# Score shift as a DMA into the queries' row, the second product ahead of it, and one power for two norms

## The chip, the cores and the metric

One core of a Trainium2 chip runs the whole kernel in one launch. The metric is the device time of an execution in microseconds (us). In the profile PE is the matrix engine, PEld its weight loads, DVE the vector engine, ACT the scalar engine, POOL the GpSimd engine, and SP the engine that here only issues DMAs. An engine's name with a q (SPq, ACTq) stands for its instruction queue.

## The reference

Four sequences of 512 tokens with 512 features go through a gated block: attention of the tokens to themselves and to a second sequence (the context), both with queries from the tokens, and then a feed-forward part. The inputs are normed twice in a row, by the block's layer norm and by that of the attention:

```python
x = x + jnp.tanh(g_xattn[0]) * _L0_xattn_ref(_layernorm(x), ctx_2048, ...)
x = x + jnp.tanh(g_ffn[0]) * _L0_ffn_ref(_layernorm(x), w_gate_up, w_down)

def _layernorm(x, axis=-1, eps=1e-05):            # the first norm
    m = jnp.mean(x, axis=axis, keepdims=True)
    v = jnp.var(x, axis=axis, keepdims=True)
    return (x - m) / jnp.sqrt(v + eps)

# in _L0_xattn_ref: d = 128, g = 8 groups of 2 query heads, s = 512
ln_out = _ln(hidden_states, ln_w, ln_b)           # the second norm, eps 1e-5 too
q = _ln(_fp8_linear_pertensor(ln_out, wq, ...).reshape(b, s, g, hpg, d), qln_w, qln_b)
k = _ln(_fp8_linear_pertensor(ln_out, wk, ...).reshape(b, s, g, d), kln_w, kln_b)
v = _fp8_linear_pertensor(ln_out, wv, ...).reshape(b, s, g, d)
core = _gqa(q, k, v).reshape(b, s, nh * d)        # the same with qx and the context's kx, vx: xout
catq = _div_clamp_fp8(jnp.concatenate([core, xout], axis=-1), proj_smooth)
return jnp.einsum('bsi,oi->bso', catq, wproj) * (proj_in_scale * proj_w_scale)

def _gqa(q, k, v):
    scores = jnp.einsum('bsghd,btgd->bghst', q, k) / np.sqrt(q.shape[-1])
    return jnp.einsum('bghst,btgd->bsghd', jax.nn.softmax(scores, axis=-1), v)
```

The feed-forward part (a projection to 2 x 2048, a silu gate, a projection back, with weights of three values) is not touched by the change.

## The kernel before

The attention is cut into 64 blocks: a kind (0 self, 1 cross), a group of two heads and a sequence. Each block has two units, one for each head; a unit is one of the 128 **steps** of the main loop, and a step has two **halves**, of 256 queries each. There are 256 halves. The projections for later blocks run in the same halves: a `Pair` is two of a block's four token tiles, and one pair is projected in each step, five steps ahead.

The scores are kept exact enough by splitting queries and keys into a high and a low fp16 part. `qk` holds, for each token tile, seven turned chunks of 128 features: two query heads and the key in high parts (0 to 2), the same in low parts (3 to 5), and the key's high part again (6). Feature 0 is kept free: row 0 of chunk 6 is all ones, so whatever stands in row 0 of a low query chunk is added to all scores of that query. This row takes minus the largest score, so the exponential can be taken without overflow and without a pass of its own.

One half `n` of a step, in the order in which `step` writes it (u0 is the unit of this half, u1 that of the half before, u2 that of two halves before; w1, w2 are projected tiles on their way):

- `scores`: eight products of PE into `ps_s` (four key tiles by 256 queries, two terms). `ps_s` has two buffers.
- `shift_put` of u1: ACT copies the shift row from `mt` in PSUM to row 0 of the query chunk.
- `top`: DVE reduces the scores over the four key tiles to `mx` (128 x 256).
- `out` of w2 (ACT and DVE norm a projected tile into `z`), `sq` of w1 (ACT sums squares into `ss`).
- `shift_mm` and `exps` of u1: four products add the low queries and the shift; ACT takes the exponential of `ps_s` into `pt`.
- `pv` of u2: the second product, into `po`.
- `top_turn`: PE turns `mx` into `mt`.
- `vals` and `var` of w1 (ACT copies the values to `vv`; DVE, then POOL's power at L559, make `ss` the reciprocal deviation), and the next tile's projections (`mm`, into `ps_p`).
- `split`, once a step: ACT casts `z` to the high part in `hl`, POOL subtracts for the low part (L586), SP issues the transpose into `qk` (L587).
- `quant` and `turn_out`, once a step: DVE quantizes `ob`, SP transposes it into `ot` (L709), and ACT stores an earlier one to `cat_d`.
- `shift`: DVE reduces `mt` to `nm`, the negated maxima, with queries on partitions. `shift_row`: two products of PE with `nm`, broadcast, turn it into a row in `mt`.
- `evac` of u2: DVE scales `po` into `ob`.

The matrix, vector and scalar engines keep this written order from step 19 (`cfg["p0"]`) to the fourth step from the end; before and after that the build orders instructions by its own estimate of times. SP and POOL are ordered by the build throughout. Other work is hung into the halves by fixed lists (`PLAN`): each entry advances a generator by one step at a given point. The lists `a1`, `a2` and `a3` advance `prep_self`, which loads a sequence (`xt`), norms it, turns it and quantizes it into `xa` and `yx` (`yb` holds the scaled values). `prep_cross` does the same for the context: SP loads `cf` (L438), POOL subtracts (L447). After the attention come the output projection (`psj`, part of it early) and the feed-forward part (`ga`, `ub`, `psd`). Line 86 of the profile is a helper that issues all instructions of PE, DVE and ACT, so tiles are named rather than lines.

Of the kernel before, what the change touches and what calls it, by code (L numbers as in the profile page):

```python
# [22 lines left out]
NT = S // 128  # L23
# [71 lines left out]
def flamingo_kernel(  # L95
# [190 lines left out]
    with attn as ph:  # L286
# [11 lines left out]
        z_tiles = [nk.tile([128, 2, 3, 128], F32, name=f"z{i}") for i in range(2)]  # L298
        for t in z_tiles:
            gp.memset(t[:, :, 0:2, 0:1], 1.0)  # L300
        hl_tiles = [nk.tile([128, 2, 7, 128], F16, name=f"hl{i}") for i in range(2)]
        for t in hl_tiles:
            gp.memset(t[:, :, 6, 0:1], 1.0)
# [17 lines left out]
        def prep_self(b):  # L321
# [15 lines left out]
            t2 = sm.tile([128, 5, NT], F32, name="t21")  # L337
            v.tensor_scalar(t2[:, 0], mv[:, :, 1], EPS, None, ALU.add)
            gp.tensor_tensor(t2[:, 1], t2[:, 0], mhalf4, ALU.pow)
            yield  # L340
            v.tensor_tensor(t2[:, 2], t2[:, 1], t2[:, 1], ALU.mult)
            yield
            v.tensor_tensor(t2[:, 2], t2[:, 2], mv[:, :, 1], ALU.mult)
            yield
            v.tensor_scalar(t2[:, 2], t2[:, 2], EPS, None, ALU.add)
            gp.tensor_tensor(t2[:, 3], t2[:, 2], mhalf4, ALU.pow)
            yield
            v.tensor_tensor(t2[:, 3], t2[:, 3], t2[:, 1], ALU.mult)
            yield
            v.scalar_tensor_tensor(t2[:, 4], mv[:, :, 0], -1.0, t2[:, 3], ALU.mult, ALU.mult)  # L350
            yield
            for tt in range(NT):
                r, m = t2[:, 3, tt : tt + 1], t2[:, 4, tt : tt + 1]
# [147 lines left out]
        class Block:  # L501
            def __init__(self, ty, g, b):
                self.ty, self.g, self.b = ty, g, b
                self.qk = qkp.tile([128, NT, 7, 128], F16, name="qk")
                self.v = v_tiles[n_blocks[0] % 4]
                n_blocks[0] += 1

        class Pair:
# [55 lines left out]
            def out(self, i):  # L564

                ty, ps, z, r = self.ty, self.ps[i], self.z[:, i], self.ss[:, i, 2]
# [12 lines left out]
            def split(self, low=None):  # L579
                z, hl = self.z, hl_tiles[self.k % 2]  # L580
                gp.tensor_tensor(  # L581
                    z[:, :, 2, 0:1], self.acc, cb[:, self.ty : self.ty + 1].broadcast_to((128, 2, 1)), ALU.add
                )
                sc.copy(hl[:, :, 0:3], z)
                gp.tensor_copy(hl[:, :, 6, 1:128], z[:, :, 2, 1:128])
                (low or gp).tensor_tensor(hl[:, :, 3:6], z, hl[:, :, 0:3], ALU.subtract)  # L586
                sy.dma_start_transpose(  # L587
                    self.qk[:, self.pr * 2 : self.pr * 2 + 2].rearrange("p t c q -> p (t c) q"),
                    hl.rearrange("p i c d -> p (i c d)"),
                )  # L590

        class Unit:
# [9 lines left out]
            def scores(self, h):  # L602
                qk, j = self.blk.qk, self.j
                ps = self.ps[h] = pp_s.tile([128, NT, 256], F32, name="ps_s")
                for t in range(NT):
                    for n, (kc, qc) in enumerate(((2, j), (5, j))):
# [3 lines left out]
                            qk[:, t, kc],  # L610
                            qk[:, 2 * h : 2 * h + 2, qc],
# [5 lines left out]
            def top(self, h):  # L617
# [4 lines left out]
                v.tensor_reduce(self.mx, self.ps[h].rearrange("p t q -> p q t"), AX.X, ALU.max)  # L622

            def top_turn(self):
                mt = pp_o.tile([128, 512], F32, name="mt", tag="rb", bufs=1)
                self.mt = mt[:, 0:128].bitcast(F16).rearrange("p (i q) -> p i q", i=2)
                self.mr = mt[:, 128:384]
# [7 lines left out]
            def shift_row(self):  # L635

                mr = self.mr
                for i in range(2):
                    pe.matmul(
                        mr[:, i * 128 : i * 128 + 128],  # L640
                        self.nm[:, i : i + 1].broadcast_to((128, 128)),
                        ident16,
                        start=True,
                        stop=True,
                    )

            def shift_put(self, h):

                sc.copy(
                    self.blk.qk[0:1, 2 * h : 2 * h + 2, self.j + 3], self.mr[0:1].rearrange("p (i q) -> p i q", i=2)  # L650
                )

            def shift_mm(self, h):
                qk, ps = self.blk.qk, self.ps[h]
                for t in range(NT):
                    pe.matmul(
                        ps[:, t],
                        qk[:, t, 6],
                        qk[:, 2 * h : 2 * h + 2, self.j + 3],
# [145 lines left out]
        def step(s, k):  # L805
# [4 lines left out]
            for h in range(2):  # L810
# [7 lines left out]
                if u1:  # L818
                    u1.shift_put(h1)
# [421 lines left out]
```

## Time and profile before

| | |
|---|---|
| time, median of 3 runs | 1761.86 us (1759.51 to 1761.88) |
| profiled execution, its own time | 1761.26 us |
| span of that execution | 1759.5 us, 40972 instructions |
| PE busy | 1672.0 us (95%) |
| DVE busy | 1324.2 us (75%) |
| ACT busy | 1052.5 us (60%) |
| POOL busy | 569.0 us (32%) |
| DMA moved | 192.25 MB |

The profile is of one execution; 1.8 us of its time lie outside the span. An engine's busy share says how long it worked, not whether the end waited for it. The chain of waits follows the work that ended last back to the start and gives each engine and tile its share of that chain. In a line of the timeline the first number is the start in us from the start of the span, the second the duration in us, then the engine, the line, the instruction, what it writes and reads, and in brackets how long the engine had been idle and who released it. In a line of the chain the second number is the time by which that work moved the end. A line of waits gives who waited for whom, the total in us, the number of times and the longest. A line of DMA issues gives the destination and source, the queue, the count, KB each, and the median time in us from issue to landing.

### The profile page before, as it was taken

How to read it: one execution, taken by the hardware profiler on the slowest of the kernel's cores; microseconds unless marked ns; L12 is line 12 of the kernel's file. 1: busy time of each engine (PE TensorE's matmuls, PEld its weight loads, DVE VectorE, ACT ScalarE, POOL GpSimd, SP SyncE). 2: the span in 40 equal slices, each digit the busy share in tenths (PEclk: the TensorE clock that was granted, in tenths of full speed). 3: DMA queues.
4: the chain of work that ended last, by engine and by line, in shares of the span. 5: the costliest groups of instructions: out<-in, count | busy, mean ns of one | idle time of the engine just before them, and what ended most of it. 6: DMA issues, size and time to landing. Idle time of an engine off the chain costs nothing.

```text
span 1759.5 us, 40972 instructions
## 1 busy us (share of the span) xinstructions
PE 1672.0 (95%) x15174; PEld 1422.4 (81%) x15174; DVE 1324.2 (75%) x3967; ACT 1052.5 (60%) x3413; POOL 569.0 (32%) x725
## 2 busy tenths in 40 slices
PE   3589888999999999999999999999999999999999
PEld 2478787999999999999999999999999987443444
DVE  7888877777777778777777777777766665679876
ACT  6655555666666667666666666666665553457443
POOL 3453333334444335543333333333333330110000
PEclk8699999999999999999999999999999999999999
DMA  4433434344544455644445544544476664984333
GB/s 149 118 67 67 85 68 86 67 89 83 97 86 83 87 91 136 142 85 103 103 103 103 109 103 109 103 109 103 91 127 115 138 130 134 290 251 114 84 72 90
DMA packets 450312, 192.25 MB, mean 109 GB/s; under 512 B 417312, under 2 KB 421440, under 8 KB 447680
## 3 DMA queue, kind: packets, MB, share of 16 engines
q1 hardware_dynamic: 366688, 141.38, 38.7%
q10 hardware_dynamic: 82992, 44.07, 9.2%
q0 software_dynamic: 432, 4.19, 1.3%
q8 instruction: 119, 1.95, 0.4%
q14 instruction: 81, 0.66, 0.1%
HBM read 84.71 MB, written 23.09 MB: 61 GB/s over the span
## 4 chain that ended last, share of the span: by engine, by line
PE 82%; DVE 9%; ACT 3%; POOL 2%; DMA 2%; issue 1%; ACTq 0%; SPq 0%; DVEq 0%; POOLq 0%
PE ps_p L86 26%; PE po L86 23%; PE ps_s L86 17%; PE psj L86 5%; PE psd L86 3%; PE mt L86 3%; PE ub L86 3%; PE ga L86 3%; DVE mx L86 1%; DVE yb L86 1%; POOL ss L559 1%; DVE ob L86 1%; ACT z L86 1%; DMA ot<-ob 1%; DVE z L86 1%
## 5 line engine op out<-in xcount | busy, mean ns | idle before, releaser
L86 PE MATMUL ps_p<-wq,xa 128*128 128x256 f16 (+1 forms) x5584 | 557.5, 256 | 21.1 <-DVE xa L86 9.5
L86 PEld LDWEIGHTS <-xa 128*128 128x128 f16 x5632 | 471.7, 99 | 65.4 <-DVE xa L86 12.1
L86 PE MATMUL po<-vv,pt 128*128 128x129 f32 x4096 | 501.9, 275 | 0.0
L86 DVE TENSOR_REDUCE mx<-ps_s 128x256 f16<-128x1024 f32 x256 | 313.2, 1224 | 246.3 <-PE ps_s L86 244.9
L86 PEld LDWEIGHTS po<-vv,pt 128*128 128x128 f32 x4096 | 478.5, 192 | 4.0 <-PE ps_s L86 0.7
L86 PE MATMUL ps_s<-qk 128*128 128x256 f16 x3072 | 386.1, 274 | 14.8 <-ACT qk L86 8.0
L559 POOL TENSOR_TENSOR ss<-ss,mhalf 128x3 f32<-128x3 f32 x256 | 221.2, 864 | 497.2 <-DVE ss L86 490.1
L86 ACT CAST qk<-mt 1x256 f16<-1x256 f32 x256 | 92.4, 361 | 431.1 <-PE mt L86 422.0
L86 PEld LDWEIGHTS <-qk 128*128 128x128 f16 x3072 | 291.0, 98 | 49.1 <-issue 10.5
L86 ACT ACTIVATE pt<-ps_s 128x1024 f32<-128x1024 f32 x256 | 256.4, 1001 | 21.0 <-PE ps_s L86 20.3
L586 POOL TENSOR_TENSOR hl<-z,hl 128x768 f16<-128x768 f32 x126 | 207.4, 1646 | 19.6 <-ACT hl L86 19.6
L86 ACT ACTIVATE jk<-ps_p 128x128 f32<-128x128 f32 x762 | 192.3, 253 | 22.5 <-PE ps_p L86 19.1
L86 ACT ACTIVATE z<-ps_p,ss 128x127 f32<-128x127 f32 x508 | 154.4, 350 | 51.3 <-POOL ss L559 51.1
L86 DVE SCALAR_TENSOR_TENSOR ob<-po,r,rsr 128x128 bf16<-128x128 f32 x512 | 155.9, 346 | 7.7
L86 ACT ACTIVATION_READ_ACCUMULATOR jk<-ps_p 128x1 f32 x762 | 142.9, 188 | 0.0
L581 POOL TENSOR_TENSOR z<-acc,cb 128x2 f32<-128x2 f32 x128 | 27.2, 213 | 337.0 <-DVE ss L86 293.3
L86 DVE TENSOR_REDUCE nm<-mt 128x2 f16<-128x256 f16 x256 | 107.4, 419 | 29.4 <-PE mt L86 29.3
L86 DVE TENSOR_SCALAR ob<-ob 128x512 bf16<-128x512 bf16 (+2 forms) x384 | 111.9, 291 | 8.3
L86 ACT CAST hl<-z 128x768 f16<-128x768 f32 x128 | 105.8, 827 | 19.3 <-POOL z L581 17.1
L86 DVE SCALAR_TENSOR_TENSOR y<-ps_p,ss,gk 128x128 f32<-128x128 f32 x254 | 87.1, 343 | 28.8 <-ACT z L86 27.9
L86 PEld LDWEIGHTS <-nt 128*128 128x128 bf16 x512 | 50.0, 98 | 65.4 <-issue 6.2
L86 PE MATMUL psj<-wp,cat 128*128 128x512 f16 x448 | 97.0, 379 | 0.0
(149 smaller groups left out, 1773.8 us busy)
## 6 DMA issues: line engine op xcount, KB each, us to landing
cat_d<-ot ACTq DMA_DIRECT2D x128, 128.0 KB, 2.0
cat<-cat_d SPq DMA_DIRECT2D x16, 1024.0 KB, 5.6
wf<-in_dram ACTq DMA_DIRECT2D x56, 256.0 KB, 4.3
wt<-in_dram ACTq DMA_DIRECT2D x48, 256.0 KB, 4.3
wt<-in_dram SPq DMA_DIRECT2D x24, 512.0 KB, 4.4
xt<-in_dram SPq DMA_DIRECT2D x32, 256.0 KB, 4.4
cf<-in_dram SPq DMA_DIRECT2D x16, 256.0 KB, 3.6
out_dram<-o SPq DMA_DIRECT2D x16, 256.0 KB, 2.0
```

The source lines that it names most:

```text
L86: ins = f(*args, **kw)
L559: gp.tensor_tensor(ss[:, 2], ss[:, 1], mhalf[:, 0], ALU.pow)
L581: gp.tensor_tensor(z[:, :, 2, 0:1], self.acc, cb[:, self.ty : self.ty + 1].broadcast_to((128, 2, 1)), ALU.add)
L586: (low or gp).tensor_tensor(hl[:, :, 3:6], z, hl[:, :, 0:3], ALU.subtract)
```

## The change

- `shift_row` and its two products go, and so does ACT's copy in `shift_put`. In its place SP issues a DMA from `nm` (128 partitions of two fp16) into row 0 of the query chunk (256 fp16 on one partition).
- So that each partition's two values are neighbours in the row, the 256 queries of a half are interleaved: `qk`, `z` and `hl` get the pair's tile index behind the chunk, and `top` writes its maxima in two runs, even and odd queries.
- In a half, `pv` of u2 comes ahead of `shift_mm` and `exps` of u1. `shift` and the put follow the turn at once, ahead of `vals`, `shift_mm`, `exps` and `var`.
- `prep_self` takes both norms in one power: with v the variance, the product of both reciprocal deviations is (v(1 + eps) + eps²)^-1/2. The generator has four steps fewer; the lists that advance it are unchanged.

```diff
--- before.py
+++ after.py
@@ -295,12 +295,12 @@
 
 
         nk = ph.enter_context(tc.tile_pool(name="nk", bufs=1))
-        z_tiles = [nk.tile([128, 2, 3, 128], F32, name=f"z{i}") for i in range(2)]
+        z_tiles = [nk.tile([128, 3, 2, 128], F32, name=f"z{i}") for i in range(2)]
         for t in z_tiles:
-            gp.memset(t[:, :, 0:2, 0:1], 1.0)
-        hl_tiles = [nk.tile([128, 2, 7, 128], F16, name=f"hl{i}") for i in range(2)]
+            gp.memset(t[:, 0:2, :, 0:1], 1.0)
+        hl_tiles = [nk.tile([128, 7, 2, 128], F16, name=f"hl{i}") for i in range(2)]
         for t in hl_tiles:
-            gp.memset(t[:, :, 6, 0:1], 1.0)
+            gp.memset(t[:, 6, :, 0:1], 1.0)
         ep = ph.enter_context(tc.tile_pool(name="ep", bufs=4))
         cp = ph.enter_context(tc.tile_pool(name="cp", bufs=2))
         sm = ph.enter_context(tc.tile_pool(name="sm", bufs=4))
@@ -334,23 +334,14 @@
             v.bn_aggr(mv[:, NT - 1], st_)
             yield
 
-            t2 = sm.tile([128, 5, NT], F32, name="t21")
-            v.tensor_scalar(t2[:, 0], mv[:, :, 1], EPS, None, ALU.add)
+            t2 = sm.tile([128, 3, NT], F32, name="t21")
+            v.tensor_scalar(t2[:, 0], mv[:, :, 1], 1.0 + EPS, EPS * EPS, ALU.mult, ALU.add)
             gp.tensor_tensor(t2[:, 1], t2[:, 0], mhalf4, ALU.pow)
             yield
-            v.tensor_tensor(t2[:, 2], t2[:, 1], t2[:, 1], ALU.mult)
-            yield
-            v.tensor_tensor(t2[:, 2], t2[:, 2], mv[:, :, 1], ALU.mult)
-            yield
-            v.tensor_scalar(t2[:, 2], t2[:, 2], EPS, None, ALU.add)
-            gp.tensor_tensor(t2[:, 3], t2[:, 2], mhalf4, ALU.pow)
-            yield
-            v.tensor_tensor(t2[:, 3], t2[:, 3], t2[:, 1], ALU.mult)
-            yield
-            v.scalar_tensor_tensor(t2[:, 4], mv[:, :, 0], -1.0, t2[:, 3], ALU.mult, ALU.mult)
+            v.scalar_tensor_tensor(t2[:, 2], mv[:, :, 0], -1.0, t2[:, 1], ALU.mult, ALU.mult)
             yield
             for tt in range(NT):
-                r, m = t2[:, 3, tt : tt + 1], t2[:, 4, tt : tt + 1]
+                r, m = t2[:, 1, tt : tt + 1], t2[:, 2, tt : tt + 1]
                 if tt % 2 if b == 0 else tt in cfg["nv"]:
                     v.tensor_scalar(zs[tt], zs[tt], r, m, ALU.mult, ALU.add)
                 else:
@@ -501,7 +492,7 @@
         class Block:
             def __init__(self, ty, g, b):
                 self.ty, self.g, self.b = ty, g, b
-                self.qk = qkp.tile([128, NT, 7, 128], F16, name="qk")
+                self.qk = qkp.tile([128, NT // 2, 7, 2, 128], F16, name="qk")
                 self.v = v_tiles[n_blocks[0] % 4]
                 n_blocks[0] += 1
 
@@ -563,7 +554,7 @@
 
             def out(self, i):
 
-                ty, ps, z, r = self.ty, self.ps[i], self.z[:, i], self.ss[:, i, 2]
+                ty, ps, z, r = self.ty, self.ps[i], self.z[:, :, i], self.ss[:, i, 2]
                 for s in range(2):
                     sc.activation(
                         z[:, s, 1:128], ps[:, s * 128 + 1 : s * 128 + 128], AF.Copy, scale=r[:, s : s + 1]
@@ -579,14 +570,14 @@
             def split(self, low=None):
                 z, hl = self.z, hl_tiles[self.k % 2]
                 gp.tensor_tensor(
-                    z[:, :, 2, 0:1], self.acc, cb[:, self.ty : self.ty + 1].broadcast_to((128, 2, 1)), ALU.add
+                    z[:, 2, :, 0:1], self.acc, cb[:, self.ty : self.ty + 1].broadcast_to((128, 2, 1)), ALU.add
                 )
-                sc.copy(hl[:, :, 0:3], z)
-                gp.tensor_copy(hl[:, :, 6, 1:128], z[:, :, 2, 1:128])
-                (low or gp).tensor_tensor(hl[:, :, 3:6], z, hl[:, :, 0:3], ALU.subtract)
+                sc.copy(hl[:, 0:3], z)
+                gp.tensor_copy(hl[:, 6, :, 1:128], z[:, 2, :, 1:128])
+                (low or gp).tensor_tensor(hl[:, 3:6], z, hl[:, 0:3], ALU.subtract)
                 sy.dma_start_transpose(
-                    self.qk[:, self.pr * 2 : self.pr * 2 + 2].rearrange("p t c q -> p (t c) q"),
-                    hl.rearrange("p i c d -> p (i c d)"),
+                    self.qk[:, self.pr].rearrange("p c i q -> p (c i) q"),
+                    hl.rearrange("p c i d -> p (c i d)"),
                 )
 
         class Unit:
@@ -607,8 +598,8 @@
 
                         pe.matmul(
                             ps[:, t],
-                            qk[:, t, kc],
-                            qk[:, 2 * h : 2 * h + 2, qc],
+                            qk[:, t // 2, kc, t % 2],
+                            qk[:, h, qc],
                             start=(t % 2 == 0 and n == 0),
                             stop=False,
                             skip_group_check=True,
@@ -619,12 +610,16 @@
 
 
                 self.mx = sm.tile([128, 256], F16, name="mx", bufs=2)
-                v.tensor_reduce(self.mx, self.ps[h].rearrange("p t q -> p q t"), AX.X, ALU.max)
+                v.tensor_reduce(
+                    self.mx.rearrange("p (i q) -> p q i", i=2),
+                    self.ps[h].rearrange("p t (q i) -> p q i t", i=2),
+                    AX.X,
+                    ALU.max,
+                )
 
             def top_turn(self):
                 mt = pp_o.tile([128, 512], F32, name="mt", tag="rb", bufs=1)
                 self.mt = mt[:, 0:128].bitcast(F16).rearrange("p (i q) -> p i q", i=2)
-                self.mr = mt[:, 128:384]
                 for i in range(2):
                     pe.transpose(self.mt[:, i], self.mx[:, i * 128 : i * 128 + 128], ident16)
 
@@ -632,22 +627,10 @@
                 self.nm = sm.tile([128, 2], F16, name="nm", bufs=4)
                 v.tensor_reduce(self.nm, self.mt, AX.X, ALU.max, negate=True)
 
-            def shift_row(self):
-
-                mr = self.mr
-                for i in range(2):
-                    pe.matmul(
-                        mr[:, i * 128 : i * 128 + 128],
-                        self.nm[:, i : i + 1].broadcast_to((128, 128)),
-                        ident16,
-                        start=True,
-                        stop=True,
-                    )
-
             def shift_put(self, h):
 
-                sc.copy(
-                    self.blk.qk[0:1, 2 * h : 2 * h + 2, self.j + 3], self.mr[0:1].rearrange("p (i q) -> p i q", i=2)
+                sy.dma_start(
+                    out=self.blk.qk[0:1, h, self.j + 3].rearrange("o a (b i) -> o (a b) i", i=2), in_=self.nm
                 )
 
             def shift_mm(self, h):
@@ -655,8 +638,8 @@
                 for t in range(NT):
                     pe.matmul(
                         ps[:, t],
-                        qk[:, t, 6],
-                        qk[:, 2 * h : 2 * h + 2, self.j + 3],
+                        qk[:, t // 2, 6, t % 2],
+                        qk[:, h, self.j + 3],
                         start=False,
                         stop=True,
                         skip_group_check=True,
@@ -815,24 +798,24 @@
                 w1, w2, w3 = [x.pop(0) if x else None for x in tiles]
                 if u0:
                     u0.scores(h0)
-                if u1:
-                    u1.shift_put(h1)
-                if u0:
                     u0.top(h0)
                 if w2:
                     w2[0].out(w2[1])
                     tiles[2].append(w2)
                 if w1:
                     w1[0].sq(w1[1])
-                if u1:
-                    u1.shift_mm(h1)
-                    u1.exps(h1)
                 if u2:
                     u2.pv(h2)
                 if u0:
                     u0.top_turn()
+                    u0.shift(h0)
+                    u0.shift_put(h0)
                 if w1:
                     w1[0].vals(w1[1])
+                if u1:
+                    u1.shift_mm(h1)
+                    u1.exps(h1)
+                if w1:
                     w1[0].var(w1[1])
                     tiles[1].append(w1)
                 if q:
@@ -846,9 +829,6 @@
                     turned.append(units.pop((n - 3) // 2))
                     if len(turned) > 1:
                         turned.pop(0).store()
-                if u0:
-                    u0.shift(h0)
-                    u0.shift_row()
                 if u2:
                     run(u2.evac(h2))
                 background(5 * s + 1 + 2 * h + LEAD)
```

## The prediction

> **What bounds the kernel now.** I read the page first: the busy slices and the share of the chain that ended last.
>
> ```profile
> PE   3589888999999999999999999999999999999999
> ...
> PE 82%; DVE 9%; ACT 3%; POOL 2%; DMA 2%; issue 1%; ACTq 0%; SPq 0%; DVEq 0%; POOLq 0%
> PE ps_p L86 26%; PE po L86 23%; PE ps_s L86 17%; PE psj L86 5%; PE psd L86 3%; PE mt L86 3%; PE ub L86 3%; PE ga L86 3%; DVE mx L86 1%; DVE yb L86 1%; POOL ss L559 1%; DVE ob L86 1%; ACT z L86 1%; DMA ot<-ob 1%; DVE z L86 1%
> ```
>
> PE carries the end. `mt`, the score maxima's turn and the row products, has 3% of the chain. Before slice 8 (about 310 us) PE isn't full, so the chain in order of time comes next, first in the full part:
>
> ```profile
> 704.93 1.31 PE ps_s L86 x12
> 706.24 1.79 PE po L86 x16
> 708.03 0.11 PE mt L86 x2
> 708.14 1.77 PE ps_p L86 x24
> 709.91 0.11 PE mt L86 x2
> ```
>
> This is one half of a step, 5.09 us, PE alone: 8 score and 4 shift products, second product (`po`), turn, projections (`ps_p`), and last the two row products, 0.11. The same pattern, with 2.18 for `ps_p` and 5.50 us in all, runs from 733.5 to 1435 in the cross blocks. The chain is PE alone from 318 on, which is where the written order begins (step 19); before that it alternates between DVE, POOL, ACT and PE. The waits of PE from 60 to 330 us say on whom:
>
> ```profile
> PE mt L86 <- DVE nm L86: 11.0, 12, 3.3
> PE ps_s L86 <- ACT qk L86: 8.0, 10, 1.1
> ```
>
> Both are the links that the change takes out: row products waiting for `nm`, shift products waiting for ACT's copy. Third, the timeline of the same half shows the distances:
>
> ```profile
> 705.40 1.29 SPq L587 DMA_TRANSPOSE qk<-hl  x1
> 705.84 1.22 DVE L86 TENSOR_REDUCE mx<-ps_s 128x256 f16<-128x1024 f32 x1 [1.09 <-PE ps_s L86]
> 706.50 1.00 ACT L86 ACTIVATE pt<-ps_s 128x1024 f32<-128x1024 f32 x1
> 707.87 0.28 PE L86 MATMUL mt<-ident,mx 128*128 128x128 f16 x2
> 708.18 0.42 DVE L86 TENSOR_REDUCE nm<-mt 128x2 f16<-128x256 f16 x1 [0.25 <-PE mt L86]
> 710.06 0.36 ACT L86 CAST qk<-mt 1x256 f16<-1x256 f32 x1 [1.60 <-PE mt L86]
> ```
>
> `mx` ends at 707.06, its turn starts at 707.87: 0.81 us to spare. Last, DMA landings, for the new transfer:
>
> ```profile
> qk<-hl SPq DMA_TRANSPOSE x128, 4.3
> ot<-ob SPq DMA_TRANSPOSE x128, 2.4
> wb<-in_dram SPq DMA_DIRECT2D x1, 768.0 KB, 6.4
> icol<-in_dram ACTq DMA_DIRECT2D x1, 8.0 KB, 3.3
> gt<-in_dram SPq DMA_DIRECT2D x1, 1.0 KB, 5.6
> rsm_d<-rr SPq DMA_DIRECT2D x1, 16.0 KB, 1.4
> ```
>
> **Row products out.** Two matmuls a half, 0.11 us of the chain. Halves in the full part: (733.5 − 318)/5.09 = 82 and (1435 − 733.5)/5.50 = 127, so 209 × 0.11 = −23.0 us, if nothing else becomes late. The new half is 4.98 (self) or 5.39 (cross): scores to 0.87, second product to 2.66, turn to 2.77, shift products to 3.21, projections to the end. ACT's 0.36 copy goes too, off the path here.
>
> **What becomes tight.** Moving the second product ahead takes the 0.44 of shift products away from `mx`'s cover: 0.81 − 0.44 = 0.37 us remain, cost 0. The new `mx` writes its 256 values in two interleaved runs, reading the same 1024; I take 1.22 again. The exponential moves from about 1.6 to 3.3–4.3 of the half; the next scores, which need its buffer, come at 4.98: 0.7 to spare, cost 0. On DVE `nm` now stands ahead of the variance and the quantization; it is ready at 707.43 + 0.31 and DVE is with `z` until 707.85, so those two wait only for its 0.42. POOL's power (0.85) follows the variance and is done before the next half's ACT `z`.
>
> **The put.** It waits on SP for `nm` (end at 3.4 of the half); queued behind it are the transposes of `ob` and `hl` and the loads, none of which is due within the half. PE's shift products wait for it, and behind them projections and next scores. They come at 4.98 + 2.77 = 7.75. Small landings of the trace, 1.4 to 2.4, give 4.8 to 5.8: on time by 2 us. The second put of a step has the `hl` transpose ahead of it on SP, and that moves later with the exponential: 4.3 + 0.83 (cast) + 1.64 (POOL) = 6.8, landing 4.3 later, 11.1. The second shift products come at 2 × 4.98 + 2.77 = 12.73 (cross 13.55), so 1.6 (2.4) us are left. How long a small transfer takes behind a big one is seen once: `wb`, issued at 4.04, lands at 10.4, and `gt`, issued at 5.48, at 11.1, so 0.7 after it. By that the put is in time by 0.9. If instead its whole 2.4 came after the landing, it would be late by 0.8 in 41 self steps and not in cross ones: 0 to +33; I take 0, by the `gt` row.
>
> The Trainium skill ("DMA: Bandwidth & Descriptors", "Queues, rings and completion order") says that an engine takes descriptors in ring order, which is the wait that `gt` shows. The same page ("Anatomy of one DMA — SWDGE (gpsimd) path") speaks against the change: about 2.0 us fixed for any size, for 512 bytes that ACT copies in 0.36; by its 2.0 the first put lands at 5.4, still before 7.75, and the sum stays.
>
> **Early stretch, 60 to 318.** Up to step 19 the build orders instructions, and the new order differs throughout. The removed links' waits are 11.0 + 8.0, and `ps_t` waited 2.4 more for ACT's copy: at most −21. In the quiet steps from 283 to 318 a half takes 5.95 us, the cast of `hl` standing ahead of the copy on ACT (308.08 in the chain, shift products behind). In the new order of those steps ACT ends with that cast, and I find nothing longer than PE's 4.98: 6 × 0.97 = −5.8. In the busier steps DVE's `yb` and POOL's powers stay on the chain; I take −1, in all −7. The other end: the generator of the next input's norm is four steps shorter, so the prologue's fixed list now reaches one more turn, four scalings (0.6 to 0.7) and a clip (0.7), +3.4 if none lies in a wait.
>
> **One power.** At the start two DVE products, an addition, a POOL power (1.02) and a further product go: `xt` can be normed near 10.7 instead of 14.11. DVE is filled with weights there, so of 3.4 only its own instructions and idle time are sure: −2 (−3.4 to 0). For the other three inputs it is inside the early term.
>
> **Loads of the cross inputs.** On SP four times four loads stand between puts, and SP waited for POOL there 16.9 us in 6 waits, 3.9 at most. A put delayed by 3.9 is late by 3.9 − 2 = 1.9: 0 to +12; I take +3, since the loads stand where the build expects them to be free.
>
> **End of attention and the layouts.** Ten halves after 1435 have no projections; their scores could wait for the later exponential: −1 to +3, taken 0. The casts and transposes move the same bytes, 0.
>
> **Sum** against the profiled execution, 1761.26 us (span 1759.5): −23 − 7 − 2 + 3 = −29, so 1732. The median, 1761.86, is 0.6 above it, the lowest 1759.51; no matter here.
>
> **Rivals.** *The second put comes late* (slower). If it lands x after the `hl` transpose, steps lose 41 (x − 1.6) + 64 (x − 2.4). This passes 29 at x = 2.4. For: 128 pieces of four bytes into one partition, no such row in the trace. Against: `gt` with x = 0.7. With `icol`'s 3.3 it is 70 + 58 = 128, so 1860. Chance 0.11.
>
> *`mx` becomes the bound* (slower). It decides from 0.37 + 29/209 = 0.51 us of extra length or delay. If the interleaved output made it half as long again (+0.61), 209 × 0.24 = +50, 1782. Against: it reads as much as before. 0.08.
>
> *The early stretch gives all* 21, not 7: 1718. For: the quiet steps. Against: DVE busy 45 of 50 us between 150 and 200. 0.10.
>
> *The early stretch gives nothing and the loads cost 12*: −23 − 2 + 3 + 12 = −10, 1751. 0.13, of which 0.04 lies within 0.2%.
>
> **How the numbers follow.** Forecast 0.58 (1722 to 1746). Faster by over 0.2% (3.5 us, what a measurement here can tell): 0.58 + 0.10 + 0.09 = 0.77; same 0.04; slower 0.11 + 0.08 = 0.19. The range reaches from the third rival, with a few us for the other bounds, to the put being late by its bound (−29 + 33, and some of the loads): 1714 to 1775; the rest of the slower cases stays out.
>
> **What would show it.** Right: the chain from about 310 on PE alone with 4.98 and 5.39 a half, `mt` at half its share, puts landing in 2 to 3 us, no PE wait for DMA `qk`. Wrong: PE `ps_s` waiting for DMA `qk<-nm` in every second half (first rival), PE `mt` waiting for DVE `mx` (second), an early stretch that ends after 318.

## The result: slower by 0.26%, and where the time went

Median of the kernel after: 1765.17 us (15 runs, 1762.59 to 1769.43). The kernel before, on the same chip: 1761.06 us (15 runs, 1758.67 to 1762.11). The ratio is 1.0026, with a 95% interval of 1.0018 to 1.0034. The forecast was 1732, so the sign is wrong and 33 us are missing. The profiled execution after has a span of 1763.9 us, against 1759.5.

The page after, in the same parts as those shown of before: the busy slices of PE, the share of the chain by engine and by line, PE's score group with what it waited for, and the new transfer in the DMA issues.

```profile
PE   3478998999999999999999999999999999999999
...
PE 73%; DVE 11%; DMA 7%; issue 4%; ACT 3%; POOL 2%; ACTq 0%; SPq 0%; DVEq 0%; POOLq 0%
PE ps_p L86 24%; PE po L86 19%; PE ps_s L86 16%; DMA qk<-nm 5%; PE psj L86 5%; PE psd L86 3%; PE ub L86 3%; PE ga L86 3%; DVE mx L86 2%; DVE yb L86 2%; PE mt L86 1%; POOL ss L550 1%; DVE ob L86 1%; DVE ms L86 1%; DVE wf L86 1%
...
L86 PE MATMUL ps_s<-qk 128*128 128x256 f16 x3072 | 422.8, 274 | 32.3 <-DMA qk<-nm 24.4
...
qk<-nm SPq DMA_DIRECT2D x256, 0.5 KB, 2.6
```

`mt` falls from 3% to 1% of the chain, as forecast, and the put lands in 2.6 us at the median. But PE now has 73% of the chain instead of 82%, and the put's flights, which count whole there, have 5%; PE itself waited 24.4 us for it. The chain in order of time, in the written order of the self blocks, shows a half as the prediction has it:

```profile
548.50 0.87 PE ps_s L86 x8
549.37 1.79 PE po L86 x16
551.16 0.11 PE mt L86 x2
551.27 0.44 PE ps_s L86 x4
551.71 1.77 PE ps_p L86 x24
```

4.98 us, and the same pattern is 5.39 in the cross blocks. The row products' 0.11 us is gained in every undisturbed half. So the loss is in a few disturbed ones. To find them I took the start of `mx` on DVE in each half from the two timelines:

| half | before, us | after, us | difference | row products alone, since the line above | lost |
|---|---|---|---|---|---|
| 2 | 92.0 | 98.3 | +6.3 | | |
| 38 | 324.1 | 317.9 | -6.2 | | |
| 100 | 639.6 | 629.4 | -10.2 | 62 x -0.11 = -6.8 | 2.8 |
| 120 | 742.3 | 735.7 | -6.6 | -2.2 | 5.8 |
| 220 | 1292.8 | 1282.1 | -10.7 | -11.0 | 6.9 |
| 240 | 1402.8 | 1403.0 | +0.2 | -2.2 | 13.1 |
| 255 | 1478.0 | 1481.5 | +3.5 | about -0.5 | 3.8 |

The last column is the measured difference from line to line less the column before it. These are single executions: in four of the runs below that leave halves 100 to 120 as they are (`wp` in chunks, cut or spread), that line loses 3.7 to 4.2 us instead of 5.8. From half 38 to half 220 the change still led by 6 to 11 us; the greatest loss, 13.1 us, lies in twenty halves near the end, from 1282 to 1403 us. PE's waits between 1290 and 1430 us have one cause, and the chain in order of time shows it at its first place:

```profile
PE ps_s L86 <- DMA qk<-nm: 10.6, 4, 3.3
```

```profile
1295.45 8.18 DMA qk<-nm
1303.63 0.04 issue
1303.67 0.60 PE ps_s L86 x4
```

A put of 512 bytes takes 8.18 us instead of 2.6. Two more like it follow, 7.94 us from 1342.09 and 9.20 us from 1390.09; the last also stands behind two loads of `cat`, 1 MB each, on SP's own queue. What else moves then is in the DMA view of 1294 to 1302 us, the packets by queue and the issues with their time to landing:

```profile
q0 software_dynamic: 124, 1.52, 102.9%
q10 hardware_dynamic: 41, 0.01, 1.0%
q1 hardware_dynamic: 35, 0.00, 0.6%
...
cat_d<-ot ACTq DMA_DIRECT2D x1, 128.0 KB, 8.8
qk<-nm SPq DMA_DIRECT2D x1, 0.5 KB, 8.2
```

q0 is the load of `wp` (L954, POOL's queue, 1.5 MB in 128 packets of 12288 bytes, about 1 us each); it fills all 16 engines of this window (102.9%), and its last packets end at 1303.1. q1 is SP's queue, with the put's four-byte pieces, and q10 is ACT's, with the store of `ot`. In the trace's packet records the first piece of the put moves at 1299.26, 3.8 us after its issue; in undisturbed first puts of a step between 1305 and 1410 it moves after 1.1 to 1.4 us. From 1300 to 1302 there are 31 packets of the put, 32 of the store and 32 of `wp`, in turn, and the rest of the put goes when `wp` is through: 35 of its 144 packets in the window, 1.52 MB of `wp` around them. The Trainium skill ("DMA: Bandwidth & Descriptors", "Queues, rings and completion order") says that a DMA engine goes round the queues that have work, one packet at a time. The equal counts from 1300 on agree. The delay before them, 2.4 us or more beyond an undisturbed put's, with `wp` alone moving, does not, and why stays open.

The kernel before has the same loads. Nothing there is due soon, so they cost it nothing; but their price stood in its trace. The DMA view of before, 1296 to 1312 us, with one of them under way:

```profile
wp<-in_dram POOLq DMA_DIRECT2D x1, 1536.0 KB, 10.8
...
cat_d<-ot ACTq DMA_DIRECT2D x1, 128.0 KB, 10.5
ot<-ob SPq DMA_TRANSPOSE x2, 5.3
qk<-hl SPq DMA_TRANSPOSE x2, 7.4
```

The transposes of `ot` and `hl`, 2.4 and 4.3 us on its page, take 5.3 and 7.4 here.

### The profile page after: what moved, and what is told of

The parts are those of the page before. It is cut to its first block, busy times and chain, and to the rows that moved or that the text cites. A ratio compares the mean times of both kernels' runs of the same rounds, so it can differ in the third digit from the quotient of the medians.

```text
span 1763.9 us, 40437 instructions
## 1 busy us (share of the span) xinstructions
PE 1649.9 (94%) x14662; PEld 1399.0 (79%) x14662; DVE 1345.2 (76%) x3951; ACT 1005.2 (57%) x3157; POOL 573.6 (33%) x721
## 4 chain that ended last, share of the span: by engine, by line
PE 73%; DVE 11%; DMA 7%; issue 4%; ACT 3%; POOL 2%; ACTq 0%; SPq 0%; DVEq 0%; POOLq 0%
PE ps_p L86 24%; PE po L86 19%; PE ps_s L86 16%; DMA qk<-nm 5%; PE psj L86 5%; PE psd L86 3%; PE ub L86 3%; PE ga L86 3%; DVE mx L86 2%; DVE yb L86 2%; PE mt L86 1%; POOL ss L550 1%; DVE ob L86 1%; DVE ms L86 1%; DVE wf L86 1%
## 5 line engine op out<-in xcount | busy, mean ns | idle before, releaser
L86 ACT ACTIVATE pt<-ps_s 128x1024 f32<-128x1024 f32 x256 | 262.0, 1024 | 496.7 <-PE ps_s L86 457.8
L86 PEld LDWEIGHTS <-xa 128*128 128x128 f16 x5632 | 483.0, 99 | 77.7 <-DVE xa L86 15.0
L86 DVE TENSOR_REDUCE mx<-ps_s 128x256 f16<-128x1024 f32 x256 | 333.7, 1304 | 253.5 <-PE ps_s L86 252.3
L86 PE MATMUL ps_s<-qk 128*128 128x256 f16 x3072 | 422.8, 274 | 32.3 <-DMA qk<-nm 24.4
L86 ACT ACTIVATE jk<-ps_p 128x128 f32<-128x128 f32 x762 | 202.8, 284 | 20.0 <-PE ps_p L86 18.4
L86 ACT ACTIVATE z<-ps_p,ss 128x127 f32<-128x127 f32 x508 | 158.6, 366 | 61.5 <-POOL ss L550 61.5
L86 ACT ACTIVATION_READ_ACCUMULATOR jk<-ps_p 128x1 f32 x762 | 163.8, 215 | 0.0
L86 PEld LDWEIGHTS <-cat 128*128 128x128 f16 x512 | 50.3, 98 | 58.4 <-issue 0.3
L86 DVE SCALAR_TENSOR_TENSOR z<-y,hk 128x128 f32<-128x128 f32 x256 | 92.4, 361 | 0.3 <-POOL hk L276 0.3
```

The lines of the kernel that those rows point to most:

```text
L86: ins = f(*args, **kw)
```

## The experiments

Theory A: the change has three faults besides its gain. The put stands on PE's path and takes 8 to 9 us beside bulk loads (13 us lost); the first norm's shorter generator puts work into the prologue (6 us at half 2); the second product ahead of the shift's pass takes `mx`'s cover (7 us). The rivals stand with each run. Times are medians of 4 to 11 runs; the ratio is to the kernel before on the same chip, with its 95% interval.

**The parts alone.** First, the kernel before with nothing but the norm in one power (the hunk of `t2` in the diff):

> The kernel before, with nothing of the change but the first norm in one power (two generator steps in place of six). Theory A (the shorter generator pushes more of the second input's norm into the prologue; the changed kernel started its second half 6.4 us later than the kernel before): the start of half 2 moves from 92.0 to 95 to 99 us, and little of it is won back, since the halves after 318 us are PE's alone: 1763 to 1768 against 1761.1. Rival (the prediction's own term: the start gains and nothing is lost): 1759 to 1760.

Measured: 1766.99 us, ratio 1.0035 (1.0023 to 1.0047). `mx` of half 2 starts at 98.7 us, and from half 38 to the end the kernel is 5.0 to 5.1 us behind before, in every half. So fewer operations at the start make the kernel slower. PE's waits between 60 and 110 us, of this run, start with two lines that the kernel after has with the same numbers:

```profile
PE ps_t L86 <- DVE psc L86: 5.7, 1, 5.7
PE ps_p L86 <- ACT yb L86: 4.6, 1, 4.6
```

`ps_t` is a turn of the second input's rows. Its wait alone is not the loss: the kernel before waits 6.0 us for such turns in this window, in two pieces (3.2 for ACT's `yb`, 2.8 for DVE's). The second line, a projection's wait of 4.6 us for ACT's `yb`, the kernel before has not; how the order of the prologue leads to it is not shown. Whether the generator's length makes half 2 late is tested with four empty steps, the arithmetic being that of after:

```
             gp.tensor_tensor(t2[:, 1], t2[:, 0], mhalf4, ALU.pow)
-            yield
+            for _ in range(5):
+                yield
```

> The changed kernel with four empty steps in the generator of the first norm, so that it has six steps as before; the arithmetic is the new one. Theory A (the 6.4 us at half 2 come from the fixed list of the prologue reaching further into the second input's norm): half 2 starts at 92 to 93 instead of 98.3, and the time is 1759 to 1762. Rival D (the same work is only moved, and was won back before 318 us): half 38 starts where it does in the changed kernel (317.9), 1764 to 1766.

Measured: 1761.82 us, ratio 1.0006 (0.9997 to 1.0014), against 1.0026 of the kernel after. Half 2 starts at 90.4, half 38 at 312.8 (after: 317.9). Theory A holds and rival D falls: the lead of 5 us at half 38 is kept to the end (at half 255 it is 0.9 ahead of the kernel before, where the kernel after is 3.5 behind). So in the kernel after the generator's length costs 3.5 us, whatever its arithmetic. Alone, on the kernel before, length and arithmetic together cost 6.2; no run separates them there.

Next, the order alone, on the kernel before:

```
-                if u1:
-                    u1.shift_mm(h1)
-                    u1.exps(h1)
                 if u2:
                     u2.pv(h2)
                 if u0:
                     u0.top_turn()
                 if w1:
                     w1[0].vals(w1[1])
+                if u1:
+                    u1.shift_mm(h1)
+                    u1.exps(h1)
+                if w1:
                     w1[0].var(w1[1])
```

> The kernel before with only the order changed: second product ahead of the shift's pass and the exponential; row products and ACT's copy stay, no DMA put, old norm. Theory A (the maximum's cover falls from 0.81 to 0.37 us, and it is late where DVE prepares weights in the background): PE waits some 6 to 9 us for mx between 770 and 1230 us and nothing is won, 1766 to 1771. Rival B (the order is free, as the prediction has it): 1760 to 1762, and PE's waits for mx stay near nothing.

Measured: 1758.48 us, ratio 0.9994 (0.9985 to 1.0002). Theory A's total is out, and the time lies a little below rival B's range; the parts are not rival B's: half 38 starts 6.6 us before the kernel before does, and of these 4.2 are lost again between halves 160 and 210. There PE waits for `mx`; this is its line for 770 to 1285 us in this run, and then in the kernel after (the kernel before has none):

```profile
PE mt L86 <- DVE mx L86: 3.2, 6, 0.7
```

```profile
PE mt L86 <- DVE mx L86: 4.3, 6, 0.9
```

So the lost cover costs, as theory A has it, but the early stretch pays for it. The early gain of the whole change, -6.2 at half 38, is no more than what the order gives by itself; but the run with the empty steps is 11.3 ahead there, so some 4.7 more were gained and 5.1 lost to the shorter generator. One of the late places, in the timeline of the kernel after:

```profile
957.38 1.65 POOL L577 TENSOR_TENSOR hl<-z,hl 128x768 f16<-128x768 f32 x1 [0.88 <-ACT hl L86]
957.64 1.40 DVE L86 SCALAR_TENSOR_TENSOR ms<-ms,sw 128x3 f32<-128x3 f32 x1
959.08 0.86 DVE L86 TENSOR_SCALAR wf<-wf,sw,ms 128x128 f32<-128x128 f32 x3
959.85 1.29 DVE L86 TENSOR_REDUCE mx<-ps_s 128x256 f16<-128x1024 f32 x1
961.20 0.28 PE L86 MATMUL mt<-ident,mx 128*128 128x128 f16 x2 [0.90 <-DVE mx L86]
```

The scores are done at 958.4, where the second product starts, but `mx` starts at 959.85, behind the weights' preparation. A product of three elements a row takes 1.40 us, and ends where POOL's 1.65 us on `hl` ends; elsewhere the same instruction takes 0.16. In the same half of the kernel before, POOL is almost through with `hl` when the product comes:

```profile
965.49 1.64 POOL L586 TENSOR_TENSOR hl<-z,hl 128x768 f16<-128x768 f32 x1
966.99 0.16 DVE L86 SCALAR_TENSOR_TENSOR ms<-ms,sw 128x3 f32<-128x3 f32 x1
968.01 1.23 DVE L86 TENSOR_REDUCE mx<-ps_s 128x256 f16<-128x1024 f32 x1
```

The product is held so in three of the six late halves of the kernel after (957.6, 1045.7 and 1133.8 us); in another, from 1002 us, a weight product of 128x512 stands ahead of `mx`. The Trainium skill ("SBUF — State Buffer", "Who interferes with whom") says that a DVE instruction with two inputs from SBUF contends with a GpSimd instruction that reads SBUF, for a shared port that is an exclusive lock; the row of 1.40 us agrees.

**The loads of `wp`.** The first question is whether they are the cause. The loads are cut to their first column, 128 KB instead of 1.5 MB, with the same work on every engine, first on the kernel after:

```
-                gp.dma_start(out=wp[i][:, 0:n], in_=wproj[:, 12 * i : 12 * i + n])
+                gp.dma_start(out=wp[i][:, 0:1], in_=wproj[:, 12 * i : 12 * i + 1])
...
-                    ps, cats[t][:, c], wp[c // 12][:, c % 12], start=(c == 0), stop=(c == NCH - 1)
+                    ps, cats[t][:, c], wp[c // 12][:, 0], start=(c == 0), stop=(c == NCH - 1)
```

> The changed kernel with the loads of wp cut to their first column each (128 KB instead of 1.5 MB; the last product uses that column throughout, so its numbers are not the reference's; the work of every engine is the same). Theory A (between 1290 and 1430 us the puts wait for wp's packets on the DMA engines, directly or behind a transpose that does): halves 223 and 231 lose under 0.5 us instead of 3.5 and 4.9, halves 238 and 239 keep what belongs to cat's load (up to 4.5); 1754 to 1757. Rival C (these puts are late for what SP has queued, not for wp): the stalls stay, 1763 to 1766.

Measured: 1752.66 us, ratio 0.9956 (0.9943 to 0.9969). Halves 223 and 231 lose nothing, half 238 loses 1.7; the lead over the kernel after grows from 2.1 us at half 223, ahead of the loads, to 13.3 at half 240. The same edit on the kernel before:

> The kernel before with the loads of wp cut to their first column (the last product uses that column throughout, so its numbers are not the reference's). Theory A (only the puts made these loads costly): 1759 to 1762, nothing won. Rival K (the loads always cost this stretch something): 1750 to 1757.

Measured: 1761.31 us, ratio 1.0005 (0.9996 to 1.0014): no change. So these loads cost 11 to 12 us with the puts and nothing without, and rivals C and K fall.

Is it the large packets? Each load in 12 DMAs of one column, 1024 bytes a row, at the same place:

```
-                gp.dma_start(out=wp[i][:, 0:n], in_=wproj[:, 12 * i : 12 * i + n])
+                for c in range(n):
+                    gp.dma_start(out=wp[i][:, c], in_=wproj[:, 12 * i + c])
```

> The changed kernel with each of the three loads of wp (12 columns of 128x512 in one DMA, 12288 bytes a row) issued as 12 DMAs of one column, 1024 bytes a row, at the same place on the same queue: the same bytes. Theory A (a put's 8 four-byte packets on each DMA engine take turns with packets of 12288 bytes, about 1 us each): the puts of 8 to 9 us between 1290 and 1430 fall to 4 or less, and some 8 to 11 of the 13 us lost there return: 1754 to 1757. Rival C (the puts wait for the bytes, whatever their packets): puts stay at 7 us or more, 1764 to 1766.

Measured: 1766.22 us, ratio 1.0031 (1.0021 to 1.0041): a miss, the time stays. The chain shows the put at the first load to be as long as before, and what led to it:

```profile
1300.85 0.21 POOL z L572
1301.06 0.34 POOL hl L576
1301.39 0.85 POOL ss L550
1302.24 0.95 SPq L578
1303.20 0.05 issue
1303.25 8.06 DMA qk<-nm
```

It is now a second put, standing on SP's queue behind the transpose of `hl` (SPq L578), whose 256-byte packets share the engines with 1024-byte ones until 1305; and POOL's issues, 12 of some 0.55 us, make POOL's own work on `hl` later. The size of the packets alone doesn't decide it.

Then the same bytes spread: one or two columns at the end of each half, and the first three loads of `cat` in four pieces.

> The changed kernel with the loads of wp issued one or two columns (128 KB) at the end of each half and the first three loads of cat in four pieces, one a step: the same bytes, spread. Theory A (it is the bursts that hold the puts): no put over 5 us between 1290 and 1430, 9 to 12 of the 13 us return: 1753 to 1757. Rival C (any byte beside the puts costs them its time): 1762 to 1768.

Measured: 1764.91 us, ratio 1.0027 (1.0017 to 1.0037). This told nothing on the burst: POOL's queue isn't in written order, and the timeline shows eight columns issued in a row from 1291.11 to 1295.6 and the rest by 1300.3. In the next run each column is tied to its half by a one-element write of DVE after `mx`, and `cat`'s pieces go on ACT's queue:

```
+        def drip(s, h):
+            n = n_steps - s
+            for _ in range(2 - h if n > 8 else 1):
+                if drops:
+                    o, src = drops.pop(0)
+                    v.memset(o[0:1, 0:1], 0.0)
+                    gp.dma_start(out=o, in_=src)
...
                     u0.top(h0)
+                drip(s, h)
```

> The spread of wp's loads again, made to hold: each column of 128 KB is tied to its half by a one-element write of DVE after mx, so that POOL can't issue the columns in a row, and the three cat loads go in four pieces each on ACT's queue, one a step. Theory A (bursts on the DMA engines hold the puts): no put over 5.5 us between 1290 and 1430, 9 to 13 of the 13 us come back, 1752 to 1757. Rival C (any byte beside the puts costs them its time, or the cast load is slow in itself): 1761 to 1768.

Measured: 1754.62 us, ratio 0.9974 (0.9963 to 0.9986), faster than both kernels. PE's waits for the put between 1285 and 1435 us, of this run:

```profile
PE ps_s L86 <- DMA qk<-nm: 1.9, 3, 0.9
```

10.6 us have become 1.9, and no put there takes over 4.91 us. It is the burst that hurts, not the bytes. Of the gain 4.1 us are lost again between halves 240 and 255, and since `cat`'s pieces moved to ACT's queue in the same run, `cat`'s share is not separated from its queue.

**The put's queue.** Is a put late because of its place on SP? On ACT's queue instead, ahead of the exponential:

```
-                sy.dma_start(
+                sc.dma_start(
                     out=self.blk.qk[0:1, h, self.j + 3].rearrange("o a (b i) -> o (a b) i", i=2), in_=self.nm
```

> The changed kernel with the puts issued on ACT's queue instead of SP's, after the values' copy and ahead of the exponential. Theory A (a put is late because it stands in SP's queue behind transposes and loads): the late second puts (3 us before 655), the losses of 655 to 740 us (7 us) and the part behind transposes between 1290 and 1430 go, 1750 to 1758. Rival E (ACT now waits for nm with the exponential behind it, 0.3 to 0.7 us later in each half, where 0.7 was to spare): PE waits for ACT at the next scores, 1765 to 1800.

Measured: 1769.01 us, ratio 1.0054 (1.0041 to 1.0066). Theory A falls here: the late second puts of the self blocks remain (0.75, 0.70 and 0.41 in halves 44, 56 and 68), and halves 223, 231 and 239 now lose 8.9, 5.2 and 7.8, with puts of 10.92, 8.20 and 10.07 us. Another queue does not get past the bulk load. Rival E is there too, but small: nearly every half between 330 and 640 us loses 0.08, its next scores starting 0.05 us after the end of the exponential that they wait for; in the kernel after 0.54 us lie between the two. The loads of `cf` on POOL's queue instead of SP's (`gp.dma_start(out=c, ...)`):

> The changed kernel with the 16 loads of cf issued by POOL instead of SP. Theory A (in 655 to 740 us a put waits on SP behind cf's issue, which waits for POOL): the loss there falls from 7 to 2 us or less, 1759 to 1762. Rival F (the loads' transfers hold the DMA engines, wherever they are issued, or POOL's issues make its powers and hl late): 1764 to 1770.

Measured: 1765.19 us, ratio 1.0023 (1.0014 to 1.0032): no change, and PE's waits for the put between 640 and 770 us are 3.3 against 3.4. So SP's order is not what the cross inputs' loads cost, and rival F is left. The chain of this run speaks for its first half, the transfers:

```profile
666.99 0.33 DVE nm L86
667.33 0.03 DVE ss L86
667.36 5.39 DMA qk<-nm
```

The put is issued as soon as `nm` is there, so nothing of POOL's made it late, and it still takes 5.39 us (5.33 in the kernel after, from 668.06). A transpose of `hl`, a weight load on ACT's queue and the load of `cf` move in that time; no run separates these three.

**The second put.** If the cast of `hl` goes ahead of the exponential on ACT, its transposes should be out of the put's way:

```
+                if w3 and w3[1]:
+                    w3[0].split()
                 if u1:
                     u1.shift_mm(h1)
                     u1.exps(h1)
...
-                if w3 and w3[1]:
-                    w3[0].split()
```

> The changed kernel with the cast of hl ahead of the exponential on ACT, where ACT waits for PE's shift products anyway: the transposes of hl are issued some 1 to 2 us earlier in the half, and the second put no longer stands behind them. Theory A (the second puts are late by their place behind hl's transposes): the losses of 0.6 to 1 us each in halves 44, 56, 68, 82, 94 and part of those of 655 to 740 us go, 3 to 8 us in all, 1757 to 1762. Rival G (the put is late by the other loads alone, or hl's transposes now meet the first put): 1763 to 1768.

Measured: 1839.83 us, ratio 1.0449 (1.0430 to 1.0467), far outside both. PE waits 74.4 us for the put. The timeline shows why:

```profile
510.20 1.65 POOL L577 TENSOR_TENSOR hl<-z,hl 128x768 f16<-128x768 f32 x1 [1.10 <-ACT hl L86]
...
510.64 1.35 DVE L86 SCALAR_TENSOR_TENSOR z<-y,hk 128x128 f32<-128x128 f32 x1
...
511.91 0.41 DVE L86 TENSOR_REDUCE nm<-mt 128x2 f16<-128x256 f16 x1
```

POOL's work on `hl` now falls on DVE's `z` (1.35 instead of 0.35), and `nm` stands behind `z`: the put is issued 1 us later, and behind the transpose as before. It shows how little the second put has to give. Two combinations, planned with this edit in them, fail with it, and say nothing good or bad of their other parts; the first adds the empty steps and the tied loads, the second moves the turn behind the shift's pass as well:

> The changed kernel with three things together: four empty steps in the first norm's generator, wp's and cat's loads spread and tied to their halves, hl's cast ahead of the exponential. If the three losses are separate and theory A holds: 1765 - 4 - 11 - 5 = 1745, between 1742 and 1750. If the cause is elsewhere (rivals C, D and G): over 1758.

> As the kernel with the three together, and the shift's pass and the exponential stand ahead of the maximum's turn, with the second product ahead of both: mx has 0.81 us of cover again instead of 0.37, and the put starts 0.44 later and is needed 0.11 earlier. Theory A (the waits of PE for mx between 770 and 1230 us come from the lost cover, and the puts now have 0.55 to give): PE's waits for mx fall from 4 to 2 us or less, 2 to 5 us better than the three together. Rival H (the puts have nothing to give): PE waits for them in most steps, 10 us or more worse.

Measured: 1877.67 us, ratio 1.0664 (1.0649 to 1.0679), and 1879.26 us, ratio 1.0696 (1.0672 to 1.0720). PE waits 98.1 and 109.7 us for the put, against 74.4 with the early cast alone. Why the added parts make that worse stays open.

**Together.** The empty steps and the tied loads:

> The changed kernel with two things together: four empty steps in the first norm's generator, and wp's and cat's loads spread and tied to their halves. If the two losses are separate (theory A): 1765 - 3.5 - 11 = 1750.5, between 1748 and 1753. If one hides the other: 1754 to 1758.

Measured: 1754.54 us, ratio 0.9963 (0.9950 to 0.9975). This is not the sum, and lies in the range for one loss hiding the other: against the tied loads alone (0.9974) the empty steps give about 2 us here, within the intervals, where they gave 3.5 to the kernel after. The next edit was meant for `mx`'s lateness:

> As the kernel with the two together, and in the second half of each step the background's weight work stands ahead of the second product's division on DVE instead of behind it. Theory I (mx is late where a background operation of DVE is held while POOL works on hl, 1.40 us for a 3-element product; 0.8 us earlier it is out of POOL's way): PE's waits for mx between 770 and 1230 us fall from 4.3 to under 2, 2 to 4 us better than the two together. Rival J (the background work is only moved, the maximum starts as late, or the second product waits for its buffer): the same within 2 us or worse.

Measured: 1753.30 us, ratio 0.9958 (0.9944 to 0.9971). It moved another planned point than that of the weights, and DVE's order is the same as in the run above, so it's a second sample of it. Moved rightly:

```
+                if h:
+                    background(5 * s + 4 + LEAD)
                 if u2:
                     run(u2.evac(h2))
...
-            background(5 * s + 4 + LEAD)
```

> As the kernel with the two together (1754), and the weight preparation of each step's end (its last planned point) stands ahead of the second product's division on DVE instead of behind it. Theory I (mx is late where an operation of DVE's weight preparation is held while POOL works on hl, 1.40 us for a 3-element product; 0.8 us earlier it is partly out of POOL's way): PE's waits for mx between 770 and 1230 us fall from 4.3 to under 2.5, 1750 to 1753. Rival J (the same work stands ahead of mx in either order, and the second product now waits for its buffer): the same or worse, 1753 to 1765.

Measured: 1765.02 us, ratio 1.0034 (1.0022 to 1.0047). Rival J: PE's waits for `mx` between 770 and 1285 us are again 4.3, and it waits for `ob` too, in every fourth half of the cross blocks (0.28 us) and more often in the self blocks. How to make room for `mx` stays open.

## Why the prediction was wrong, step by step

**Row products out (-23).** Right: 4.98 and 5.39 us in the undisturbed halves, PE's busy time down by 22.1 (1672.0 to 1649.9).

**What becomes tight (0).** Mis-sized. The new `mx` takes 1.304 us at the mean, not 1.224: the interleaved write costs 0.08, so by this difference the cover in the quiet half is 0.29, not 0.37. More: the sum moved PE's products and took DVE's timeline as it stood. In the kernel before `mx` ends 0.80 us ahead of its turn in every half from 120 to 220, so `mx` is late in none. In the kernel after, in every eighth half from 160 to 200, the weights' preparation stands ahead of `mx`, which starts about 1 us late, and nothing of the cover is left; the run with the order alone waits for `mx` in as many halves. These six halves lose 5.4 of the 6.9 us between 120 and 220. This is the second rival's mechanism, with its price in a few halves instead of all 209.

**The put (0).** The margin was right away from bulk loads: the first put is on time, the second in nearly all quiet steps, 2.8 us lost in the self blocks. The shortest put takes 1.9 us, near the 2.0 that the prediction quotes, which its source gives for DMAs that GpSimd issues; the median is 2.6. In the half from 553.5 the `hl` transpose's packets run to 558.8 and the put's go in the same last 0.5 us, straight behind them, as the `gt` row had it. The first rival is out. That there was hardly anything to spare shows where `nm` came 1 us later (the cast ahead of the exponential).

**Loads of the cross inputs (+3).** This step failed. It priced SP's queue and nothing else: where another load holds the DMA engines, the put waits wherever it is queued. The 5.8 us between halves 100 and 120 are of the size of the 3, but the run with `cf` off SP shows that SP's order is not their reason. And the loads of `wp` and `cat`, which are issued much later, were not priced at all: 13.1 us, the largest single term of the 33 that the forecast is off. Their price was in the trace of before, as shown above. The question "what else is on the engines while the put flies" was asked of the queue and not of the engines.

**Early stretch (-7).** -6.2 at half 38, near the forecast by luck: with the empty steps it is -11.3. Of that the order alone gives 6.6, with the row products and the copy in place, so the rest of the change, with the links removed, is left with some 4.7, by difference; and the shorter generator takes 5.1 back. The bound of +3.4 for the shorter generator was the right worry at half its size: 6.3 at half 2.

**One power (-2).** Wrong in sign: alone it costs 5 us in the profile and 0.35% in time. The list of the prologue counts generator steps, and in the kernel after the empty steps alone give 5.1 us back at half 38.

**End of attention (0).** 3.8 between halves 240 and 255, somewhat over the bound of +3; the order alone lost 2.2 in the last twelve halves. The rest of it stays open, as do the 0.9 us behind half 255.

With what was measured: -22.7 (the column of the table) - 6.2 + 2.8 + 5.8 + 6.9 + 13.1 + 3.8 + 0.9 = +4.4, the difference of the spans. The sum was right on the gain and took four covers for granted that the new order and the bulk loads use up in a few halves.

## What to carry to other kernels

When a small transfer takes a place on the critical path, look at every bulk load of the trace that may run beside it, and price it by what other small transfers take in that window, not by its median. When a move takes half of a cover away, ask what else the move shifts into the half that is left: here the cover was the same in every half before, and six halves used it up after. When steps of a hand-counted schedule disappear, the schedule shifts: a shorter generator is a change of order, and its cost has to be read at the end of the stretch that it reorders.

## What the runs showed of the hardware

- A 512-byte DMA that takes 2.6 us at the median takes 8.18 and 7.94 us beside a load of 1.5 MB on POOL's queue, and 9.20 behind two loads of 1 MB on its own queue and beside a third; issued from ACT's queue it takes 10.92, 8.20 and 10.07 at these loads. With the load cut into 128 KB pieces issued in a row, a put behind a transpose took 8.06 beside it; with the pieces spread over the halves, 4.91 at most.
- POOL's 1.65 us on `hl` holds two-operand DVE instructions on SBUF: 1.40 us for a 128x3 product that takes 0.16 alone, 1.35 for the 128x128 `z` that takes 0.35.
- A maximum over 128x1024 whose 256 results are written interleaved in two takes 1.304 us instead of 1.224, reading the same.
